# Fixed places for the experts' matmul groups beside the scans, and slots of their own for each kind of chunk

## The chip, the core and the metric

The kernel runs on one core of a Trainium2 chip. The metric is device time in microseconds (us) of one execution. A core has five engines with a queue each: TensorE (PE, matmuls), VectorE (DVE), ScalarE (ACT), GpSimd (POOL) and SyncE (SP, which issues most DMAs). Each takes its queue in order; a waiting instruction holds up all behind it.

## The reference: what is computed

The input is 2 batches x 256 channels x 4096 positions, float32. Layer 0 is a group norm and a Mamba block with 256 inner channels. Layer 1 is a layer norm and two Mamba blocks with 512 inner channels each, one over reversed time, and after them a mixture of 8 experts with softmax weights. The parts that matter, cut:

```python
# Mamba block: projections, causal conv of 4 taps, then a scan over time for 16 states per channel
xs, z = split(x @ W_in);  xs = silu(conv(xs))
dt = softplus(dbc[..., :16] @ W_dt + b_dt);  B, C = dbc[..., 16:32], dbc[..., 32:]   # dbc = xs @ W_x
h[t] = h[t-1] * exp(dt[t] * A) + dt[t] * xs[t] * B[t]
y = sum_s(h * C) + xs * D;  out = (y * silu(z)) @ W_out
# experts, each for every position, weighed by a softmax over mean features
h = relu(bn(x @ W1[e]));  h = relu(bn(h @ W2[e]));  y = sum_e w[e] * (h @ Wo[e] + bo[e])
```

## The kernel before

**Chunks, quads and slots.** Time is cut into 8 chunks of 512 positions. The six Mamba jobs run one after another: batch 0 layer 0 ("narrow"), batch 0 forward, batch 0 backward, then the same three of batch 1. A narrow chunk has 2 blocks of 128 channels, a forward or backward ("wide") chunk 4. The scans of a block are done in 4 quads of 2 scans each, and one scan is one **slot**: 16 slots in a narrow chunk, 32 in a wide one, 1280 in all. A place in a chunk is called p0 to p15 or p0 to p31 here; `n` is the quad modulo 8 and `h` the half, so p = 2n + h in a narrow chunk.

**What a slot holds.** In each slot ACT makes the decays of the next slot (`emit_decay`, line 752, two ACTIVATEs into PSUM, after a small join, line 763), DVE scans (`emit_scan`, line 778) and, unless `on_pool`, multiplies the states by C (line 787). POOL makes the scans' input (`emit_b`, line 742, 128x2048) and for some quads multiplies by C (line 803). PE sums the states into `y` (`emit_sum`, line 811) in the slots that `SUMS` names; `emit_skip` (818) opens a `y`, `emit_gate` (824) closes it.

**What lies beside the scans.** The next chunks are prepared in the same slots, by a table of slots relative to a chunk's start, `SLOTS`: the `xs` products (458) and their ACT copies (515), the convolution `conv` (531, tanh 540, DVE 544), `dbc` (559), `dt` (582, three ACTIVATEs 589 to 591, DVE 594, POOL 598, two stores), the gate's product `z` (458, tanh 621, DVE 624), and the out products of the chunk just scanned, `out` (841, 843, ACT copy 858, store 859). `preload_act_table_set` (660) switches ACT's table between the logarithm's and the tanh's set. `norm` does layer 1's layer norm for the forward jobs, `features` the one ahead of the experts, once a backward chunk is out. Batch 1's narrow chunks are prepared during batch 0's forward chunks and kept in DRAM (`AHEAD_SLOTS`). All these products use a pool of three PSUM banks (`psp`); a product whose bank is not yet read waits for the bank's reader.

**The experts' items.** When a chunk's features are there, its 8 experts can run. One item is (batch, chunk, expert): three layers (line 992) of two groups, a group being two matmuls that run as four passes, with an ACT step each (1005, 1001). `experts` is a planner: it walks over all slots, keeps estimates of PE's and ACT's arrears (`behind`, `act_behind`, against `PE_ROOM`, `PE_BEHIND`, `ACT_ROOM`, `ACT_BEHIND`), and puts up to five groups in a slot if the arrears, the layers' order (`follows`) and the three banks (`fits`) allow it. Groups are emitted in the queue `pe2`, behind the slot's sums. What is left when the scans end is computed in a second stage, the **tail** (`layer`, 1326, and `last_layer`, 1350), where DVE also weighs and adds the items that were computed early (1275, 1276).

**Order.** `Slots` keeps a list of functions for each slot and queue; the main loop runs, slot by slot, `sp`, then `pe`, the sums, `pe2`, the carry and decays, `act`, `dve0`, the scan, `dve`, and `pool`. `in_order` fixes this order on every engine. Weights of a layer of an item are asked for on SP 3 slots after the last use of their buffer by the item before.

Of the kernel before, what the change touches and what calls it, by code (L numbers as in the profile page):

```python
# [64 lines left out]
SUMS = {(0, 0): (-1,), (2, 0): (0, 1), (4, 0): (2, 3), (6, 0): (4,), (7, 0): (5, 6)}  # L65
# [7 lines left out]
    2: dict(xs=(-23, -22), conv=(-20,), dbc=-16, dt=(-14, -13), z=(-10, -9), out=(7, 8)),  # L73
    4: dict(
        xs=(-31, -30, -24, -23), conv=(-26, -21), dbc=-17, dt=(-15, -13, -11, -9), z=(-6, -5, -3, -2),
        out=(16, 18),
    ),
}
AHEAD = 3
AHEAD_SLOTS = dict(x=-7, scale=-5, xs=(-1, 0), conv=(2,), dbc=10, dt=(14, 22), z=(-4, 12))  # L80
# [5 lines left out]
PE_ROOM, PE_BEHIND = 3.8, 2.5  # L86
ACT_ROOM, ACT_BEHIND = 2.6, 1.2
# [5 lines left out]
class Scan:  # L93


    def __init__(self, params, din, batch, layer, flip):
        self.params, self.din, self.nj = params, din, din // P
        self.batch, self.layer, self.flip = batch, layer, flip

# [6 lines left out]
class Slots:  # L106


    QUEUES = ("sp", "pe", "act", "dve0", "dve", "pool", "pe2")

    def __init__(self):
        self.at = {}

        self.products, self.acts, self.banks = {}, {}, []

    def count(self, slot, products=0, acts=0, banks=()):
        self.products[slot] = self.products.get(slot, 0) + products
        self.acts[slot + 1] = self.acts.get(slot + 1, 0) + acts
        self.banks.extend((slot, slot + n, 1) for n in banks)
# [17 lines left out]
def hybrid_kernel(ctx: ExitStack, tc: tile.TileContext, a: dict, out: bass.AP):  # L137
# [56 lines left out]
    with ExitStack() as st:  # L194
# [159 lines left out]

        def norm(i):
# [83 lines left out]
            late = 1 if NCH < i < 2 * NCH else 0  # L439
            for d, queue, fn in (  # L440
                (-48, "sp", load_x), (-44, "pe", mean), (-43, "dve", centre), (-42, "act", square),
                (late - 41, "pe", variance), (late - 40, "act", roots), (late - 39, "dve", divide), (late - 39, "pool", add),
                (-35 if c else -38, "act", affine), (-34, "sp", store),
            ):

                sl.put(s0 + d + (6 if c == 0 else 0), queue, fn)
            s0 += 6 if c == 0 else 0
            sl.count(s0 - 44, 2, 0, (1,))
            sl.count(s0 - 43, 0, 1)
            sl.count(s0 - 41, 2, 4, (2,))  # L450
            sl.count(s0 - 40, 0, 0, (1,))
            sl.count(s0 - (36 if c else 39), 0, 2.3)
# [11 lines left out]
        def prepare(i):  # L464

            (job, c), ck, tag, s0 = steps[i], cks[i], tags[i], starts[i]
            nj, at = job.nj, SLOTS[job.nj]
            if NCH < i <= 2 * NCH + 1:
                at = dict(at, xs=(-31, -29, -24, -23), log=-18)
            ahead = job is jobs[AHEAD]  # L470
            at_rows = slice(XC, 2 * XC) if ahead else slice(0, XC)
# [49 lines left out]
            def conv(jp):  # L521
                v, th = {}, {}

                def pe():
                    for r in range(2):
                        v[r] = psp.tile([P, T], F32, tag="ps", name=f"conv_{tag}_{jp}{r}")

                    for k in range(5):
                        for r, col, j in TILES:
                            rows = slice(64 * r, 64 * r + 64)  # L530
                            nc.tensor.matmul(  # L531
                                v[r][64 * col : 64 * col + 64, :], job.matrices["conv"][rows, 2 * jp + j, k, :],
                                ck["xs", jp][rows, j, k : k + T] if k < 4 else one_col[rows, :].to_broadcast([P // 2, T]),
                                start=(k == 0), stop=(k == 4),
                            )

                def act(r):
                    j = 2 * jp + r
                    th[r] = wk.tile([P, T], F32, tag="th", name=f"thx_{tag}_{j}", bufs=3)
                    nc.scalar.activation(th[r], v[r], AF.Tanh)  # L540

                def dve(r):
                    j = 2 * jp + r
                    nc.vector.scalar_tensor_tensor(
                        of_chunk("xc", j, 6, "eh1"), th[r], 1.0, v[r], ALU.add, ALU.mult
                    )

                return (
                    (0, "pe", pe), (1, "act", lambda: act(0)), (2, "act", lambda: act(1)),
                    (2, "dve0", lambda: dve(0)), (3, "dve0", lambda: dve(1)),  # L550
                )
# [25 lines left out]
            def softplus(j):  # L577
# [22 lines left out]
                def store(key):  # L600
# [7 lines left out]
                    (0, "pe", pe), (1, "act", act), (2, "dve", dve), (2, "pool", pool),  # L608
# [3 lines left out]
            def gate(j):  # L612

                v = {}

                def pe():
                    v["ps"] = in_proj(job, ck, 1, j, f"z_{tag}_{j}")

                def act():
                    v["th"] = wk.tile([P, T], F32, tag="th", name=f"thz_{tag}_{j}", bufs=3)  # L620
                    nc.scalar.activation(v["th"], v["ps"], AF.Tanh, scale=0.5)

                def dve():
                    nc.vector.scalar_tensor_tensor(  # L624
                        of_chunk("sz", j, 8, "eu"), v["th"], 1.0, v["ps"], ALU.add, ALU.mult
                    )

                return (0, "pe", pe), (1, "act", act), (2, "dve", dve)
# [5 lines left out]
            if c == 0:  # L634
                load_weights(job, tag, s0)
                sl.put(s0 + SLOTS[nj]["xs"][0], "act", lambda: start_job(job, tag))
# [10 lines left out]
            for j in range(nj):  # L647
                put(at["xs"][j], xs(j))
                sl.count(s0 + at["xs"][j], 2, 1, (1,))
                put(at["dt"][j], softplus(j))  # L650
                sl.count(s0 + at["dt"][j], 1, 3, (2,))
                sl.count(s0 + at["z"][j], 2, 1, (2,))
            for jp in range(nj // 2):
                put(at["conv"][jp], conv(jp))
                sl.count(s0 + at["conv"][jp], 5, 1, (1, 2))
                sl.count(s0 + at["conv"][jp] + 1, 0, 1)
            put(at["dbc"], x_proj())
            sl.count(s0 + at["dbc"], nj, 1, (1,))
            for slot, table in () if ahead else ((at.get("log", at["dt"][0]), "natural_log_exp_and_others"), (at["z"][0], "exp_and_others")):
# [166 lines left out]
        def finish(i):  # L826
# [25 lines left out]

            slots = SLOTS[2 if i == AHEAD * NCH - 1 else job.nj]["out"] if i + 1 < len(steps) else (3, 4)
            for slot in slots:
                sl.count(s0 + slot, 1 + job.nj, 1, (1,))
            for m, slot in enumerate(slots):
                sl.put(s0 + slot, "pe", lambda m=m: project(m))
# [5 lines left out]
        def features(b, c, v, s0):  # L863
# [29 lines left out]
            for d, queue, fn in (  # L893
                (0, "pe", mean), (1, "dve", centre), (2, "act", square), (4, "pe", variance),
                (5, "act", lambda: rsqrt(v["var"], v["var"], eps5)), (6, "dve", divide),
                (7, "sp", lambda: nc.sync.dma_start(nf_dram[b][:, c, :, :], v["cen"])),
            ):
                sl.put(s0 + d, queue, fn)
            sl.count(s0, 2, 0, (1,))
            sl.count(s0 + 1, 0, 2)  # L900
            sl.count(s0 + 4, 2, 2, (2,))
            ready.append((s0 + 9, b, c))
# [24 lines left out]
        def experts():  # L927

            last = 2 * nq + 15
# [11 lines left out]
            def sums_in(slot):  # L941
                n, h = divmod(slot % 16, 2)
                return 1.25 * len(SUMS.get((n, h), ())) + (1 if (n, h) in ((2, 0), (6, 0)) else 0)

            todo = [(at, b, c, e) for at, b, c in sorted(ready) for e in range(E)]
            behind = act_behind = 0.0
            times = [[], [], []]

            def follows(l):
# [4 lines left out]
                waits = [(l - 1, k * KC + 1, 2)] if l else []  # L954
# [11 lines left out]
            for slot in range(last):  # L966
                behind = max(0.0, behind) + sl.products.get(slot, 0) + sums_in(slot) - PE_ROOM
                act_behind = max(0.0, act_behind) + sl.acts.get(slot + 1, 0) - ACT_ROOM
                for l in (2, 1, 1, 0, 0):
                    at = follows(l)  # L970
                    if at is None or slot < at:
                        continue
                    if behind + 2 > PE_BEHIND or act_behind + 1.3 > ACT_BEHIND or not fits(slot):
                        break
                    banks.insert(sum(b[0] <= slot for b in banks), (slot, slot + 1, 0))
                    times[l].append(slot)
                    behind += 2
                    act_behind += 1 if l == 2 else 1.3
# [4 lines left out]
            emit_experts(put)  # L983

        def emit_experts(put):
# [40 lines left out]
            for b, c, e, times in put:  # L1026
# [5 lines left out]
                sl.put(times[0], "pe2", lambda b=b, c=c, key=key: key.update(n=n[b, c]))  # L1032
                for l, (x, dst) in enumerate((("n", "h1"), ("h1", "h2"), ("h2", "u"))):
                    at = before.get(l, times[0] - 6) + 3
                    sl.put(at, "sp", lambda l=l, e=e, key=key: load_w(l, e, key["tag"]))
                    for m in range(KC):
                        slot = before[l] = times[l * KC + m]
                        pe, act = layer(x, dst, l, m, e, key)
                        sl.put(slot, "pe2", pe)
# [49 lines left out]
        at_first = SLOTS[2]["xs"][0] - 3  # L1089
# [15 lines left out]
        for g in range(nq):  # L1105
            i, jp, n = quads[g]
            for h in range(2):
# [3 lines left out]

                if (n, h) in ((2, 0), (6, 0)):
# [17 lines left out]
                if (n, h) in ((1, 0), (5, 0)) and done:  # L1130
                    emit_gate(*done.pop(0))
# [450 lines left out]
```

## Time and profile before

| what | us |
|---|---|
| median of 3 runs (lowest, highest) | 4978.65 (4976.32, 4984.62) |
| the profiled execution's own time | 4972.65 |
| its span, first to last instruction | 4970.9 |
| first scan starts, last scan ends | 58.1, 4439.8 |
| starts of batch 0 forward, backward | 525.8, 1418.9 |
| starts of batch 1 narrow, forward, backward | 2280.1, 2710.6, 3580.5 |

The page gives busy time by engine, the span in 40 slices, the chain that ended last and the costliest groups of instructions. The stages' borders are the starts of their first scans, counted off in the timeline of DVE (the scans are line 778). A view by windows gives each engine's busy time between two moments, the number of its instructions, and the share of TensorE's clock that was granted; a window's length less an engine's busy time is its idle time.

### The profile page before, as it was taken

How to read it: one execution, taken by the hardware profiler on the slowest of the kernel's cores; microseconds unless marked ns; L12 is line 12 of the kernel's file. 1: busy time of each engine (PE TensorE's matmuls, PEld its weight loads, DVE VectorE, ACT ScalarE, POOL GpSimd, SP SyncE). 2: the span in 40 equal slices, each digit the busy share in tenths (PEclk: the TensorE clock that was granted, in tenths of full speed). 3: DMA queues.
4: the chain of work that ended last, by engine and by line, in shares of the span. 5: the costliest groups of instructions: out<-in, count | busy, mean ns of one | idle time of the engine just before them, and what ended most of it. 6: DMA issues, size and time to landing. Idle time of an engine off the chain costs nothing. (4 is left out here: it accounts for less than half of the span.)

```text
span 4970.9 us, 47346 instructions
## 1 busy us (share of the span) xinstructions
PE 4225.8 (85%) x14912; PEld 1476.1 (30%) x14912; DVE 4567.6 (92%) x3097; ACT 3613.1 (73%) x7304; POOL 4340.4 (87%) x1424
## 2 busy tenths in 40 slices
PE   5777777788776899989999899889868989999999
PEld 1222222222222233333333333333222333334444
DVE  6998999999999999999999999999999999975565
ACT  5777777777777788878788788888767888862232
POOL 6998999999999999999999999999999999960000
PEclk8778899989988999999999999999989999999999
DMA  5455454444444455446676555555534455536653
GB/s 193 158 184 171 154 171 158 158 145 155 164 157 148 173 183 177 165 174 237 241 246 222 170 173 170 189 169 190 175 121 153 165 187 176 186 131 233 226 168 127
DMA packets 335407, 875.26 MB, mean 176 GB/s; under 512 B 36314, under 2 KB 111860, under 8 KB 293172
## 3 DMA queue, kind: packets, MB, share of 16 engines
q1 hardware_dynamic: 326164, 835.39, 48.7%
q0 software_dynamic: 8992, 36.85, 2.9%
q8 instruction: 118, 1.93, 0.2%
q14 instruction: 133, 1.09, 0.1%
HBM read 673.27 MB, written 198.84 MB: 175 GB/s over the span
## 5 line engine op out<-in xcount | busy, mean ns | idle before, releaser
L742 POOL TENSOR_TENSOR bq<-rxdt,bc 128x2048 f32<-128x2048 f32 x640 | 2893.8, 4544 | 15.2 <-DMA rxdt<-xdtd 7.3
L752 ACT ACTIVATE da<-rdt,w_a 128x512 f32<-128x512 f32 x2560 | 1756.9, 686 | 70.0 <-DVE bq L778 23.6
L778 DVE TENSOR_TENSOR_SCAN da<-da,h_state,bq 128x1024 f32<-128x1024 f32 x664 | 1557.9, 2346 | 50.3 <-ACT da L752 34.7
L803 POOL TENSOR_TENSOR bq<-bq,bc 128x2048 f32<-128x2048 f32 (+1 forms) x280 | 1180.1, 4215 | 22.6
L778 DVE TENSOR_TENSOR_SCAN bq<-da,h_state,bq 128x1024 f32<-128x1024 f32 x456 | 1059.0, 2338 | 8.1 <-ACT da L752 7.9
L811 PE MATMUL y<-bq,stack 128*32 128x512 f32 x5120 | 742.2, 665 | 276.5 <-POOL bq L803 251.2
L787 DVE TENSOR_TENSOR bq<-da,bc 128x1024 f32<-128x1024 f32 x760 | 926.2, 1219 | 15.7
L992 PE MATMUL e<-eh,ew 128*128 128x512 f32 x1376 | 659.5, 613 | 43.3 <-DVE sp L594 14.4
L797 ACT COPY h_state<-da 128x2 f32<-128x2 f32 x759 | 119.0, 157 | 618.8 <-DVE bq L787 615.4
L763 ACT ACTIVATE bq<-h_state,bq,a 128x1 f32<-128x1 f32 x1120 | 430.0, 384 | 4.7 <-POOL bq L742 4.1
L811 PEld LDWEIGHTS y<-bq,stack 128*32 128x32 f32 x5120 | 140.6, 116 | 823.7 <-POOL bq L803 373.6
L458 PE MATMUL z<-nx,w_in 128*128 128x512 f32 x640 | 332.6, 650 | 59.3 <-DVE q L423 21.0
L992 PEld LDWEIGHTS e<-eh,ew 128*128 128x128 f32 x1376 | 247.7, 191 | 450.4 <-issue 240.5
L531 PE MATMUL conv<-xs,w_conv 64*64 64x512 f32 x2560 | 334.6, 603 | 22.7 <-ACT xs L515 20.4
L992 PE MATMUL e<-en,ew 128*128 128x512 f32 x688 | 324.8, 605 | 26.5 <-DVE xr L891 17.6
L458 PE MATMUL xs<-nx,w_in 128*128 128x512 f32 x640 | 318.9, 626 | 31.2 <-DVE sz L624 18.4
L1330 ACT ACTIVATE h<-hp,of,sc 128x512 f32<-128x512 f32 x168 | 130.6, 777 | 275.2 <-PE hp L1326 273.7
L843 PE MATMUL o<-sz,w_out 128*128 128x512 f32 x640 | 295.8, 601 | 0.0
L1005 ACT ACTIVATE eh<-e,of,sc 128x512 f32<-128x512 f32 x344 | 260.1, 768 | 47.3 <-PE e L992 46.9
L598 POOL TENSOR_TENSOR xdt<-sp,xc 128x512 f32<-128x512 f32 x160 | 203.2, 1274 | 43.6 <-DVE sp L594 43.6
L778 DVE TENSOR_TENSOR_SCAN da<-da,bq 128x1024 f32<-128x1024 f32 x96 | 219.4, 2285 | 2.6 <-issue 1.5
L458 PEld LDWEIGHTS z<-nx,w_in 128*128 128x128 f32 x640 | 125.1, 205 | 262.1 <-issue 147.8
(145 smaller groups left out, 4753.5 us busy)
## 6 DMA issues: line engine op xcount, KB each, us to landing
rxdt<-xdtd SPq DMA_DIRECT2D x160, 1024.0 KB, 6.0
rdt<-dtd SPq DMA_DIRECT2D x160, 1024.0 KB, 6.8
bc<-bcd SPq DMA_DIRECT2D x384, 256.0 KB, 3.2
ew<-in_W SPq DMA_DIRECT2D x172, 256.0 KB, 4.9
u<-u SPq DMA_DIRECT2D x86, 512.0 KB, 5.7
u<-eu SPq DMA_DIRECT2D x82, 512.0 KB, 4.4
dtd<-sp SPq DMA_DIRECT2D x160, 256.0 KB, 3.3
xdtd<-xdt SPq DMA_DIRECT2D x160, 256.0 KB, 3.4
```

The source lines that it names most:

```text
L458: nc.tensor.matmul(ps, job.matrices["in", half][:, k, j * P : (j + 1) * P], rhs, start=(k == 0), stop=(k == KC - 1),)
L531: nc.tensor.matmul(v[r][64 * col : 64 * col + 64, :], job.matrices["conv"][rows, 2 * jp + j, k, :], ck["xs", jp][rows, j, k : k + T] if k ...
L742: nc.gpsimd.tensor_tensor(bq[g], ck["rxdt", j], over_groups(ck["bc", 0, sg]), ALU.mult)
L752: nc.scalar.activation(da[g, h][:, k, :], cks[i]["rdt", j][:, q, :], AF.Exp, scale=steps[i][0].w["a"][:, j, q * SG + sg : q * SG + sg + 1],)
L763: nc.scalar.activation(bq[g][:, q, 0:1], job.h[:, j, sg, q : q + 1], AF.Identity, scale=cks[i]["a0", j][:, h, sg : sg + 1], bias=bq[g][:, ...
L778: nc.vector.tensor_tensor_scan(b if on_pool(g, h) else d, d, b, job.h[:, j, sg, 2 * h : 2 * h + 1] if c else 0.0, ALU.mult, ALU.add,)
L787: nc.vector.tensor_tensor(bq[g][:, two, :], d, cks[i]["bc", 1, sg].rearrange("p (o t) -> p o t", o=1).to_broadcast([P, 2, T]), ALU.mult,)
L803: nc.gpsimd.tensor_tensor(b, b, cks[i]["bc", 1, sg].rearrange("p (o t) -> p o t", o=1).to_broadcast([P, groups, T]), ALU.mult,)
L811: nc.tensor.matmul(y[i, j][q * CG : (q + 1) * CG, :], stack, bq[g][:, q, :], start=False, stop=(sg == SG - 1),)
L843: nc.tensor.matmul(v[m], job.w["out"][:, j, m * P : (m + 1) * P], ck["sz", j], start=False, stop=(j == job.nj - 1),)
L992: nc.tensor.matmul(ps, ew[l][:, k, m * P : (m + 1) * P], key[x][:, k, :], start=(k == 0), stop=(k == KC - 1),)
L1005: nc.scalar.activation(key[dst][:, m, :], key["ps", l, m], AF.Relu, bias=of[:, l, e, m : m + 1], scale=sc[:, l, e, m : m + 1],)
```

## The change

Fixed tables take the planner's place, and each kind of chunk has tables of its own.

- `PLACES` says for each kind of chunk how many groups a slot may hold, and by its sign where: negative in a new queue `pe1` ahead of the slot's sums and other products, positive in `pe2` behind them. The order of layers and the three banks still decide, too. The estimates of arrears and their `count`s are gone; `hold` keeps the banks' part.
- `SLOTS` is now by kind. Narrow: `xs` a slot earlier (-24, -23), `conv` a slot earlier, the second `dt` a slot later, `z` at (-8, -9) in place of (-10, -9), `out` at (6, 9) in place of (7, 8). Forward: `z` in the order (-6, -3, -5, -2), `out` two slots later. Backward: the last `z` four slots later, at +2. The switch to tanh's table has a slot of its own, `tanh`. Batch 0's forward chunks 1 to 7 and backward chunks 0 and 1 keep the old slots (`UNDER_AHEAD`).
- `norm` of batch 1's forward chunks 1 to 7 is one to two slots earlier (`NORM`); `features` has its square one slot later and its store two.
- `WHEN`, `GATES` and `APART` name values that stay as they were.

```diff
 SLOTS = {
-    2: dict(xs=(-23, -22), conv=(-20,), dbc=-16, dt=(-14, -13), z=(-10, -9), out=(7, 8)),
-    4: dict(
-        xs=(-31, -30, -24, -23), conv=(-26, -21), dbc=-17, dt=(-15, -13, -11, -9), z=(-6, -5, -3, -2),
-        out=(16, 18),
-    ),
+    "l0": dict(xs=(-24, -23), conv=(-21,), dbc=-16, dt=(-14, -12), z=(-8, -9), tanh=-6, out=(6, 9)),
+    "fwd": dict(xs=(-31, -30, -24, -23), conv=(-26, -21), dbc=-17, dt=(-15, -13, -11, -9), z=(-6, -3, -5, -2), tanh=-3, out=(18, 20)),
+    "bwd": dict(xs=(-31, -30, -24, -23), conv=(-26, -21), dbc=-17, dt=(-15, -13, -11, -9), z=(-6, -5, -3, 2), tanh=-4, out=(16, 18)),
 }
+UNDER_AHEAD = dict(xs=(-31, -29, -24, -23), conv=(-26, -21), dbc=-17, log=-18, dt=(-15, -13, -11, -9), z=(-6, -5, -3, -2), tanh=-6, out=(16, 18))
+NORM = (-50, -45, -44, -43, -42, -41, -40, -34, -32)
+NORM_0 = (-48, -44, -43, -42, -40, -39, -38, -35, -34)
+FIRST_NORM = (-43, -38, -37, -36, -35, -34, -33, -32, -29)
+FEATURES = (0, 1, 3, 4, 5, 6, 9)
+PLACES = {
+    "l0": (1, 1, 0, -2, 1, -2, -1, -2, 0, 0, 2, 1, 0, 1, 2, 0),
+    "fwd": (1, 1, 1, 1, 1, 0, 2, -2, 1, 0, 1, 1, -1, 2, 1, 1, -1, -2, 2, -1, 2, 0, -1, 1, 1, 1, 1, 1, 1, 1, 1, 1),
+    "bwd": (1, 1, 1, 1, 1, 0, 1, 1, -1, 1, 1, 0, 1, 1, 0, 1, 1, -1, 1, 1, 2, -1, 2, -1, -1, -1, 1, 0, 1, -2, 1, -1),
+}
...
-            for slot, table in () if ahead else ((at.get("log", at["dt"][0]), "natural_log_exp_and_others"), (at["z"][0], "exp_and_others")):
+            for slot, table in () if ahead else ((at.get("log", at["dt"][0]), "natural_log_exp_and_others"), (at["tanh"], "exp_and_others")):
...
-            for slot in range(last):
-                behind = max(0.0, behind) + sl.products.get(slot, 0) + sums_in(slot) - PE_ROOM
-                act_behind = max(0.0, act_behind) + sl.acts.get(slot + 1, 0) - ACT_ROOM
-                for l in (2, 1, 1, 0, 0):
-                    at = follows(l)
-                    if at is None or slot < at:
-                        continue
-                    if behind + 2 > PE_BEHIND or act_behind + 1.3 > ACT_BEHIND or not fits(slot):
-                        break
...
+            for i, (job, _) in enumerate(steps):
+                for p in range(8 * job.nj if i + 1 < len(steps) else 8 * job.nj + 15):
+                    slot = starts[i] + p
+                    free = abs(PLACES[job.kind][p]) if p < 8 * job.nj else 1
+                    for l in (2, 1, 1, 0, 0):
+                        at = follows(l)
+                        if at is None or slot < at:
+                            continue
+                        if not free or not fits(slot):
+                            break
+                        banks.insert(sum(b[0] <= slot for b in banks), (slot, slot + 1, 0))
+                        times[l].append(slot)
+                        front[slot] = p < 8 * job.nj and PLACES[job.kind][p] < 0
+                        free -= 1
...
-                        sl.put(slot, "pe2", pe)
+                        sl.put(slot, "pe1" if front[slot] else "pe2", pe)
...
                 sl.run(slot, "sp")
                 flush(slot)
 
+                sl.run(slot, "pe1")
                 if (n, h) in ((2, 0), (6, 0)):
                     emit_skip(i, 2 * jp + n // SG)
                 sl.run(slot, "pe")
```

## The prediction, as it was put on record

> **What bounds it now.** I read the page first, then idle time by stage, then who ended the waits in the two narrow stages, then one narrow chunk in order of time, and last the chain that ended last.
>
> ```profile
> span 4970.9 us, 47346 instructions
> PE 4225.8 (85%) x14912; PEld 1476.1 (30%) x14912; DVE 4567.6 (92%) x3097; ACT 3613.1 (73%) x7304; POOL 4340.4 (87%) x1424
> ```
>
> The table by windows (columns: window, its length, then busy time with number of instructions of PE, weight loads, DVE, ACT, POOL, then granted clock, DMA share, GB/s) has the six jobs and the tail:
>
> ```profile
> 58.10:525.80 467.70, 327.89 (x1168) 101.77 (x1168) 443.79 (x305) 342.86 (x704) 441.92 (x143) 0.81 0.52 177
> 525.80:1418.90 893.10, 696.10 (x2766) 216.32 (x2767) 877.49 (x600) 686.27 (x1435) 879.91 (x292) 0.90 0.48 159
> 1418.90:2280.10 861.20, 743.82 (x2743) 255.16 (x2742) 846.60 (x546) 677.38 (x1388) 855.55 (x271) 0.94 0.48 169
> 2280.10:2710.60 430.50, 397.02 (x1285) 145.83 (x1284) 407.08 (x241) 349.03 (x705) 417.68 (x127) 0.96 0.70 241
> 2710.60:3580.50 869.90, 782.63 (x2870) 268.39 (x2868) 855.36 (x557) 712.28 (x1453) 861.55 (x278) 0.96 0.54 176
> 3580.50:4439.80 859.30, 736.37 (x2704) 253.84 (x2700) 842.85 (x540) 669.57 (x1369) 846.07 (x269) 0.94 0.46 161
> 4439.80:4970.90 531.10, 510.81 (x1266) 222.56 (x1264) 276.23 (x274) 150.19 (x201) 28.78 (x41) 0.99 0.55 186
> ```
>
> Length less busy gives POOL's idle time: 25.8, 13.2, 5.7, 12.8, 8.4 and 13.2 us in the six jobs (7.9 of the last at its very end), DVE's: 23.9, 15.6, 14.6, 23.4, 14.5, 16.5. Both engines are full at once, and the change takes none of their instructions away in the scans. So a better order can win only idle time. A steady backward chunk (window 4120.0 to 4227.8) has 0.6 idle on POOL and 1.2 on DVE, and 9.8 on PE: nothing to win there. The tail is PE's: 510.81 of 531.10.
>
> **The tail: +10.6.** Laid side by side, the two programs' orders of instructions hold 86 and 85 early items (516 and 510 groups). One more is left to the tail. Its price is a round of the chain that ended last:
>
> ```profile
> 4562.49 4.29 PE hp L1326 x10
> ...
> 4569.63 3.43 PE y L1350 x8
> 4573.07 4.29 PE hp L1326 x10
> ```
>
> 4573.07 - 4562.49 = 10.58 us for one item's 24 passes. DVE loses 2 x 1.2 us of adding an early item and gains one weighing; it is idle for half of the tail, so neither counts. Behind the last scan come 10 groups in place of 9. A group is 4 passes of 0.43, 1.7 us, but PE waits 2.2 us for the tail's first weights there; I take 0 (to +1.7).
>
> **Batch 0's narrow chunks: +6.** No experts run here; only the slots move. In the chunk at 286.4, in order of time:
>
> ```profile
> 312.96 0.58 ACT L858 COPY xr<-o 128x512 f32<-128x512 f32 x1
> 313.38 0.67 DVE L624 SCALAR_TENSOR_TENSOR sz<-thz,z 128x512 f32<-128x512 f32 x1
> 314.11 2.07 PE L841 MATMUL o<-xr,ident 128*128 128x512 f32 x2 [7.44 <-DVE sz L624]
> 318.62 0.59 ACT L858 COPY xr<-o 128x512 f32<-128x512 f32 x1 [1.66 <-PE o L843]
> 320.37 3.70 PE L458 MATMUL xs<-nx,w_in 128*128 128x512 f32 x8
> 322.39 0.59 ACT L515 COPY xs<-xs 128x512 f32<-128x512 f32 x1 [1.33 <-PE xs L458]
> 324.66 2.36 DVE L778 TENSOR_TENSOR_SCAN da<-da,h_state,bq 128x1024 f32<-128x1024 f32 x1 [0.40 <-issue]
> ```
>
> The second out product stands 7.44 us until DVE has read a z bank; it ends at 318.51; ACT, in order, waits for it and for the xs product, so the decay of p12 is late and the scan waits 0.40 (1.17 in the chunk before). After the change the z readers are on p9 and p10. Without a reader on p8, scan 9 starts at 314.5 and its reader ends at 314.5 + 2.26 + 0.67 = 317.4. The out product then takes 4.4 as here (314.11 to 318.51) or 2.6 as its sister did without a pause before it (302.21 to 304.79), and ends at 321.9 or 320.0. On p10 ACT has its copy (0.59), the table load, now on p10 (1.28), and the one xs copy that is left (0.59 + 0.20 for the edges; its product ends 1.85 after the out product), then join and decays (1.6): 326.2 or 324.4. The scan of p12 is due at 324.2 (scans 9, 10 and 11 with their followers: 3.98 + 3.46 + 2.26). It is 2.0 or 0.2 late, against 0.4 to 1.2 now. The convolution, a slot earlier, only follows. The difference lies between -1.0 and +1.6 a chunk; PE still pauses before that product and the granted clock of this chunk is 0.78, so I go toward the slow row: +1.0 in 6 chunks, +6 (-6 to +10).
>
> [...]
>
> **Batch 1's narrow chunks: -5.** The first six hold 15 to 19 groups each today, 12 after; the last two 11 and 7, then 11 and 3. PE goes from 397 of 430.5 busy to about 397 - 35 x 1.7 = 337. DVE's waits in this stage are for decays that ACT makes late behind PE:
>
> ```profile
> DVE da L778 <- ACT da L752: 13.9, 15, 4.9
> ```
>
> The longest, 4.9, comes from a group that waits 4.8 for its last layer's weights; such loads are asked for 3 slots after the buffer's last use, and reuse after only 4 slots occurs 60 times today, 22 times after. But POOL idles only 12.8 here, 8.0 of it in the last two chunks, which hardly change. The most is 12.8 less 8 half-steady chunks at 0.3 = 10.4. I take 5 (from -10 to +3, if late groups now meet the same spots).
>
> **Wide chunks: -1.** Steady chunks hold 18 groups before and after; only places move, with PE idle 9.8 a chunk, so 0. Batch 1's first two backward chunks go from 1 and 0 groups to 19 and 16; PE idles 33 and 32 us in them, the 34 groups cost 58, and the like chunks of batch 0 (108.0 with 18 groups) are not longer than these (104.9 and 110.9): 0 (-1 to +4). The last chunk of both backward jobs goes from 33 groups to 26: -1 (-4 to 0). Batch 1's forward norm spreads the four root steps away from a softplus on the same slot: 0 (-3 to +5).
>
> **Queues.** ACT gets 31 more table loads, 111 for 80, for tanh now comes before its switch and the switch then loads the same set again: 31 x 1.283 = 39.8 us of ACT time. In the backward chunk the second load meets a wait of 1.31 us for DVE before a carry (at 1947.66) and the first is the old one moved, so I take 0; the narrow one is counted above; with the cover gone it is 40. [...]
> On SP, `out` moves the store of the residual into the slot where the next one is loaded into the same buffer (p11 narrow, p22 forward). SP then stands until the store has landed, 3.1 us in 24 chunks, with softplus stores and `bc`, `rxdt`, `rdt` loads behind it. These are asked for 9 to 12 slots (30 us and more) ahead and land in 3 to 7: 0; uncovered, 74. The norm's load and the features' store only move along empty slots.
>
> **Sum.** 10.6 + 6 - 5 - 1 = +10.6. On the profiled execution: 4972.65 + 10.6 = 4983.3. That execution is 6.0 under the median of the runs, so I put it on the median: 4978.65 + 10.6 = 4989.3.
>
> **Rivals.** Measurement can tell about 0.2%, 10 us.
> A, the sum above, chance 0.40; own range +4 to +20, about a third of it under +10.
> B, faster: the waits in both narrow stages and at the borders of jobs go. The idle time over the steady level is 23 (batch 0 narrow), 10 (batch 1 narrow) and some 4 elsewhere; two thirds of it, 25, less 10.6: -14, 4964. For it: those waits are ACT behind PE, and the change takes groups out of there. Against: batch 0's narrow chunks have none. It decides if the narrow stages shorten by over 20. Chance 0.28.
> C, slower by more: the same SP and ACT additions come through. All narrow chunks at their slow end (+10), a third of the table loads (13), -3 elsewhere and the tail: +31, 5010. It decides if DVE idles over 1.6 in a steady wide chunk. Chance 0.13.
> D, no difference: the tables name places, but layer order, buffers and banks decide as before, and what the tail costs the narrow chunks of batch 1 give back: 0, 4979. Chance 0.19.
>
> Faster 0.28 (B); same 0.19 + 0.14 of A = 0.33; slower 0.26 + 0.13 = 0.39. The range leaves out B's far third (0.09) and most of C (0.1): 4960 to 5003.
>
> **What would show it.** The last scan's end: A has it at about 4439.8 + 0, B before 4420, C after 4455. The tail from there: 531 to 542. Narrow stages: 467.7 becomes 474, 430.5 becomes 425; B has 450 and 420. DVE's idle in steady wide chunks stays at 1 to 2. The out product's wait for `sz` in a narrow chunk shrinks from 7.4 to about 2. I am wrong if the tail grows by less than 8, or if a stage of wide chunks moves by over 5.

## The result, and the profile after

The changed kernel takes 4986.76 us (median of 20 runs, 4981.08 to 4997.69) against 4978.61 (20 runs) for the kernel before on the same chip: ratio 1.0017, 95% interval 1.0010 to 1.0024. That is 8 us slower, and just under the 0.2% named as the bound. The profiled execution's span is 4979.3 us, 8.4 more than before.

The page's first lines: PE, DVE and POOL are as busy as before. ACT has 37 us more: its table loads are 130 for 99, of 1.283 us each.

```profile
span 4979.3 us, 47353 instructions
...
PE 4229.9 (85%) x14912; PEld 1462.2 (29%) x14912; DVE 4564.4 (92%) x3096; ACT 3650.0 (73%) x7333; POOL 4340.2 (87%) x1424
```

The table by windows, same columns as before, cut at the changed kernel's own borders:

```profile
58.40:517.10 458.70, 327.86 (x1168) 95.41 (x1168) 444.02 (x305) 353.82 (x712) 440.19 (x143) 0.84 0.53 181
517.10:1414.20 897.10, 703.41 (x2767) 216.68 (x2768) 877.97 (x601) 686.53 (x1435) 880.25 (x292) 0.89 0.47 159
1414.20:2278.50 864.30, 738.21 (x2723) 247.94 (x2721) 846.28 (x546) 680.44 (x1388) 857.68 (x271) 0.94 0.48 166
2278.50:2698.90 420.40, 346.85 (x1144) 120.62 (x1144) 405.97 (x241) 328.79 (x672) 413.20 (x127) 0.94 0.66 225
2698.90:3565.60 866.70, 780.32 (x2886) 272.77 (x2887) 854.36 (x556) 725.05 (x1465) 862.18 (x278) 0.97 0.54 180
3565.60:4431.60 866.00, 775.12 (x2820) 267.37 (x2818) 842.53 (x540) 695.10 (x1406) 847.40 (x269) 0.97 0.49 168
4431.60:4979.30 547.70, 526.32 (x1288) 229.05 (x1288) 275.29 (x273) 153.41 (x205) 28.88 (x41) 0.98 0.52 179
```

Both narrow stages are shorter (467.7 to 458.7, 430.5 to 420.4), both backward stages longer (861.2 to 864.3, 859.3 to 866.0), the tail longer by 16.6. One profile each can mislead, so here is every stage over all profiles that share it, the experiments' too. Terms of the change are differences of these means:

| stage | before, 2 profiles | changed, mean (profiles; lowest, highest) | difference | predicted |
|---|---|---|---|---|
| batch 0 narrow | 467.7, 467.2 | 459.3 (9; 458.6, 461.3) | -8.1 | +6 |
| batch 0 forward | 893.1, 897.7 | 898.1 (12; 895.6, 900.5) | +2.7 | |
| batch 0 backward | 861.2, 860.0 | 865.7 (8; 864.1, 868.3) | +5.1 | wide in all: -1 |
| batch 1 narrow | 430.5, 433.9 | 420.8 (9; 419.3, 422.6) | -11.4 | -5 |
| batch 1 forward | 869.9, 870.0 | 868.1 (9; 866.7, 869.6) | -1.8 | |
| batch 1 backward | 859.3, 859.1 | 867.4 (6; 862.2, 871.5) | +8.2 | |
| tail | 531.1, 535.1 | 545.3 (7; 541.5, 547.7) | +12.2 | +10.6 |

The sum is some +6.8. The difference of batch 0's forward stage is within what two profiles of the same kernel differ by.

How the out product's wait in batch 0's narrow stage went is seen in the chunk at 282.6, in order of time:

```profile
312.55 0.58 ACT L633 ACTIVATE thz<-z 128x512 f32<-128x512 f32 x1
312.94 0.67 DVE L636 SCALAR_TENSOR_TENSOR sz<-thz,z 128x512 f32<-128x512 f32 x1
...
313.66 1.13 PE L852 MATMUL o<-xr,ident 128*128 128x512 f32 x2 [1.41 <-DVE sz L636]
314.63 1.88 PE L854 MATMUL o<-sz,w_out 128*128 128x512 f32 x4
...
316.34 1.88 PE L471 MATMUL xs<-nx,w_in 128*128 128x512 f32 x4
...
317.15 1.28 ACT L671 ACT_TABLE_LOAD   x1
...
320.93 2.36 DVE L789 TENSOR_TENSOR_SCAN da<-da,h_state,bq 128x1024 f32<-128x1024 f32 x1 [0.50 <-issue]
```

The second out product waits 1.41 us for `sz`, not 7.44. After so short a pause it takes 2.85 us (313.66 to 316.51, granted clock 1.00) in place of 4.40 (0.62); xs follows at once. This chunk still comes out even, 54.7 us for 54.6: its scan of p12 is 0.50 late, for 0.40 before. Counted by chunk over the nine profiles, the -8.1 is -2.1, -0.5, +0.1, -1.2, +0.4, -2.9, -2.0 and 0.0. In chunks 0, 1 and 3 the scan of p12 had been 1.2 to 1.3 late. In chunk 5 the shorter wait counts most. There the product `mean` of `norm` stands in PE's queue behind the out and the xs products, and DVE waited for it, first before, then after:

```profile
368.67 2.08 PE L841 MATMUL o<-xr,ident 128*128 128x512 f32 x2 [7.43 <-DVE sz L624]
...
378.50 1.88 PE L399 MATMUL mean<-nx,columns 128*128 128x512 f32 x4
...
380.41 1.22 DVE L404 TENSOR_TENSOR nx<-nx,mean 128x1024 f32<-128x1024 f32 x1 [2.34 <-PE mean L399]
...
371.62 1.98 PE L416 MATMUL mean<-nx,columns 128*128 128x512 f32 x4
...
373.75 1.19 DVE L421 TENSOR_TENSOR nx<-nx,mean 128x1024 f32<-128x1024 f32 x1
```

In chunk 6 DVE's wait for the convolution's tanh falls from 3.5 to 2.1.

The chain that ended last still goes round in the tail in 10.58 us an item (4613.00 - 4602.42):

```profile
4602.42 4.29 PE hp L1332 x10
...
4609.57 3.43 PE y L1356 x8
4613.00 4.29 PE hp L1332 x10
```

### The profile page after: what moved, and what is told of

The parts are those of the page before. It is cut to its first block, busy times and chain, and to the rows that moved or that the text cites. A ratio compares the mean times of both kernels' runs of the same rounds, so it can differ in the third digit from the quotient of the medians.

```text
span 4979.3 us, 47353 instructions
## 1 busy us (share of the span) xinstructions
PE 4229.9 (85%) x14912; PEld 1462.2 (29%) x14912; DVE 4564.4 (92%) x3096; ACT 3650.0 (73%) x7333; POOL 4340.2 (87%) x1424
## 5 line engine op out<-in xcount | busy, mean ns | idle before, releaser
L997 PE MATMUL e<-eh,ew 128*128 128x512 f32 x1360 | 674.2, 625 | 54.4 <-DVE xc L556 18.9
L997 PE MATMUL e<-en,ew 128*128 128x512 f32 x680 | 336.0, 619 | 48.6 <-DVE xr L901 21.7
L829 PE MATMUL y<-xc,w_d 128*128 128x512 f32 x320 | 182.3, 653 | 29.5 <-DVE sz L835 29.5
```

The source lines that it names most:

```text
L997: nc.tensor.matmul(ps, ew[l][:, k, m * P : (m + 1) * P], key[x][:, k, :], start=(k == 0), stop=(k == KC - 1),)
```

## The experiments

Ratios are to the kernel before, run on the same chip. Stage times are from one profile each.

**The kernel before, again.** No edit.

> The kernel before once more, for a second profile: how far do its stages scatter? Four kernels with the changed kernel's tail (two items more or none apart) had tails of 541.5, 543.0, 546.2 and 547.7 us. Theory A: the kernel before scatters in the same way, so its tail is anywhere from 530 to 537 and the change's own step in the tail is the one item, 10.6 (536.6 by the mean of the other four less 544.6). Theory B: the tail of before is steady at 531 (530 to 532) and the change costs some 13 to 14 there, more than the item. For batch 0's forward stage (893.1 here, 896.6 to 900.4 in five profiles of kernels with the changed order, though its slots are the same): within 1 us of 893 if the change did something there, 896 or more if it is scatter.

Tail 535.1, batch 0 forward 897.7. Theory A: both scatter by 4 us in one and the same kernel. Seven tails of 85 items have a mean of 545.3, so the change costs 12.2 there.

**Old slots for batch 0's narrow chunks.**

```diff
+L0_0 = dict(xs=(-23, -22), conv=(-20,), dbc=-16, dt=(-14, -13), z=(-10, -9), tanh=-10, out=(7, 8))
...
         def kind_of(i):
+            if i < NCH:
+                return L0_0
```

> The changed kernel with batch 0's narrow chunks alone given back their old slots (all of them: xs, conv, dt, z, out, and the table switch on the slot of the first z); the experts' places and all other jobs stay as changed. Theory: the 9.0 us that batch 0's narrow stage lost (467.7 to 458.7) come from the new slots of z and out, which let the second out product run soon after a busy stretch; then this stage goes back to 467 (465 to 470), all other stages stay within 3 us, and the whole is about 9 us over the changed kernel (4988 of profiled span). Rival 1: the 9 us are scatter between two executions, since the stage holds no experts; then it stays at 459 (457 to 461). Rival 2: it is the earlier xs and conv that did it; this run does not tell it from the theory, a further one would.

The stage is back, to a tenth. By windows, this kernel:

```profile
59.10:526.60 467.50, 327.27 (x1168) 102.17 (x1168) 443.66 (x305) 343.87 (x705) 441.17 (x143) 0.81 0.52 176
```

The granted clock falls from 0.84 to 0.81 with it, but e5_one_load has 0.81 too and keeps 458.6, so the mean clock of the stage doesn't tell where the time goes. Rival 1 is out. The whole came to 1.0022 (1.0014 to 1.0031), 2.5 us over the changed kernel's ratio and not 9; the two intervals leave room up to 8. The stage is settled by this, the whole is not: this profile's batch 1 backward stage (862.2) and tail (541.5) are the lowest of their kind, and I can't say whether by chance.

**Only z, switch and out old there.**

```diff
+L0_0 = dict(xs=(-24, -23), conv=(-21,), dbc=-16, dt=(-14, -12), z=(-10, -9), tanh=-10, out=(7, 8))
```

> The changed kernel with only z, the table switch and out of batch 0's narrow chunks at their old slots; xs, conv and dt stay a slot earlier or later, as changed. Theory: these alone made the 9 us, so the stage is back at 466 to 468 (e1_old_narrow_b0, with all slots old: 467.5). Rival: xs and conv, a slot earlier, made part of it; then it lies between 460 and 465.

477.0, outside both: with the new xs and conv the old z and out cost 18 us, more than the old set as a whole. The waits of that stage in this kernel (engine, line, waited for: us in total, times, longest):

```profile
DVE sz L838 <- PE y L825: 11.4, 5, 3.3
DVE da L792 <- POOL h_state L816: 6.0, 5, 1.4
...
PE o L855 <- DVE sz L639: 25.7, 5, 5.5
```

The out product waits 25.7 us in all for `sz` (42.5 in the kernel before, 6.3 in the changed one), and DVE's gate now waits 11.4 us for the sums of `y` (2.6 before). I take it that the conv, a slot earlier, stands with the out product ahead of these sums. So the gains of single edits don't add: the new xs, conv and dt alone cost 9.5 us (467.5 to 477.0), the new z, switch and out on top of them win 18. The new z and out with the old xs and conv were not run, so how the 8.1 are shared isn't shown.

**One table switch.** Two kernels: `tanh` on the slot of the first z product, a slot ahead of the first tanh; and on the slot of the first tanh itself.

```diff
-    "l0": dict(xs=(-24, -23), conv=(-21,), dbc=-16, dt=(-14, -12), z=(-8, -9), tanh=-6, out=(6, 9)),
+    "l0": dict(xs=(-24, -23), conv=(-21,), dbc=-16, dt=(-14, -12), z=(-8, -9), tanh=-9, out=(6, 9)),
...
```

The first has `tanh` at -9, -6 and -6 in narrow, forward and backward chunks, the second at -8, -5 and -5.

> The changed kernel with the switch to tanh's table put on the slot of the first tanh again in all three kinds of chunk, so that 31 table loads fall away (80 in place of 111, 39.8 us of ACT time); nothing else moves. Theory, as predicted: they are hidden beside waits of ACT; every stage stays within 2 us and the whole within 3 us of the changed kernel. Rival: ACT is short in the backward stages, and the 6.6 us that batch 1's backward stage gained are these loads; then both backward stages fall by 3 to 7 us, the forward one of batch 1 by 0 to 3, and the whole is 6 to 15 us under the changed kernel.

> The changed kernel with the switch to tanh's table on the slot of the first tanh and just ahead of it: the order of all engines is that of the changed kernel, and only table loads fall away (net 30 of 130 on the page's count of all loads, 30 x 1.283 = 38.5 us of ACT time). In e2_one_switch the switch stood a slot earlier still, so that run mixed two things. Theory, as predicted: the loads are hidden, and the whole is within 3 us of the changed kernel; batch 0's narrow stage stays at 458 to 460, so that the 5.3 us of e2_one_switch there came from the earlier slot of the switch. Rival: ACT is short where the second load stands; then batch 0's narrow stage and the backward stages fall by 2 to 5 us each.

1.0019 (1.0009 to 1.0029) and 1.0019 (1.0010 to 1.0028): as the changed kernel. In the second, where nothing else moves, batch 0's narrow stage stays at 458.6, and no stage is shorter than in the other profiles of the table (900.5 and 871.5 are the longest of theirs): 38.5 us of loads were hidden, as predicted. In the first, batch 0's narrow stage is 464.0: a switch one slot too early costs 5 (in three chunks the scan interval at p8 goes from 2.26 to 3.36), a load too many nothing.

**All groups behind.**

```diff
-                        front[slot] = p < 8 * job.nj and PLACES[job.kind][p] < 0
+                        front[slot] = False
```

> The changed kernel with every place of an experts' group behind the slot's sums and products; none stands ahead of them. Number, slots and items stay as they are. Theory: the side counts little, since TensorE idles in every stage; each stage stays within 3 us of the changed kernel, and the whole within 5. Rival: a group behind a product that waits for a PSUM bank waits with it, and ACT's step for it comes too late for the next decays; then batch 1's narrow stage rises from 420.5 to 425 or more, and the two wide stages of batch 1 by 5 us each: 10 to 25 us over the changed kernel.

1.0024 (1.0015 to 1.0034); 421.1, 866.9 and 870.5 in batch 1's stages: the theory. The sign in the table is worth nothing measurable; the slots stayed as they were.

**Old wide slots, new places.**

```diff
-    "fwd": dict(xs=(-31, -30, -24, -23), conv=(-26, -21), dbc=-17, dt=(-15, -13, -11, -9), z=(-6, -3, -5, -2), tanh=-3, out=(18, 20)),
-    "bwd": dict(xs=(-31, -30, -24, -23), conv=(-26, -21), dbc=-17, dt=(-15, -13, -11, -9), z=(-6, -5, -3, 2), tanh=-4, out=(16, 18)),
+    "fwd": dict(xs=(-31, -30, -24, -23), conv=(-26, -21), dbc=-17, dt=(-15, -13, -11, -9), z=(-6, -5, -3, -2), tanh=-6, out=(16, 18)),
+    "bwd": dict(xs=(-31, -30, -24, -23), conv=(-26, -21), dbc=-17, dt=(-15, -13, -11, -9), z=(-6, -5, -3, -2), tanh=-6, out=(16, 18)),
```

> The changed kernel with the old slots of z, out and the table switch in batch 1's forward chunks and in the backward chunks; places, norm and features stay as changed. The items come out at 84 in place of 85, with 8 groups after the last scan in place of 10. Theory: the new wide slots are worth little, about -1 to +1 us in batch 1's forward stage and 0 in the backward ones; the tail grows by 10.6 for the item and loses some 3 for two groups: the whole is 5 to 10 us over the changed kernel. Rival: the backward z at +2 is what makes the backward stages longer (batch 1's from 859.3 to 862 to 869 in five profiles); then both backward stages fall by 3 to 6 and the whole comes out even with the changed kernel.

1.0098 (1.0085 to 1.0112). Both were wrong. The backward stages stay long (866.5, 866.0), so their slots are not the cause. Batch 1's forward stage grows by 25.7; in its chunks 1 to 6 DVE waits for

```profile
DVE sz L835 <- PE y L822: 12.3, 6, 2.1
DVE da L789 <- ACT da L763: 10.7, 13, 1.4
```

once 2 us a chunk for the last sum of a `y`, and then for decays; it is p18 that grows, from 3.99 to 7.67. The new places put groups on p15 and p16, and the old out products stand on p16 and p18. So the new places go with the new slots. Which of z, switch and out it is, this run doesn't tell, for it moved them together. The tail with 84 items is 556.9.

**Crowded narrow chunks.**

```diff
-    "l0": (1, 1, 0, -2, 1, -2, -1, -2, 0, 0, 2, 1, 0, 1, 2, 0),
+    "l0": (1, 1, 1, -2, 1, -2, -1, -2, 1, 1, 2, 1, 1, 1, 2, 1),
```

> The changed kernel with a place in every slot of the narrow chunks (the five zeros of the table become ones): batch 1's first six narrow chunks hold 16 to 20 groups in place of 12, and what they take is missing in batch 1's first two backward chunks (0 in place of 19 and 16). Early items stay 85, so the tail stays. Theory: the 10.1 us that batch 1's narrow stage lost come from fewer groups there; then it goes from 420.5 back to 429 or more, and batch 1's first two backward chunks lose the 4.7 us that they gained; the whole is 4 to 8 us over the changed kernel. Rival: the places (none beside the out products, none beside the carries) count and not the number; then the narrow stage comes out at 421 to 424, and the whole falls by 2 to 5 us.

1.0083 (1.0071 to 1.0095): the stage takes 455.6, 35 more. The direction is the theory's, the size is four times what I expected. Waits in this stage:

```profile
DVE da L789 <- ACT da L763: 20.2, 13, 8.3
DVE bq L789 <- ACT da L763: 16.9, 10, 4.0
...
PE e L997 <- DMA ew<-in_Wo: 18.8, 9, 7.8
PE e L997 <- DMA ew<-in_W: 14.6, 2, 9.0
```

PE waits 33 us for the experts' weights, ACT in order behind it, and DVE 37 us for ACT. The changed kernel has 7.5 and 6.6 of these. Batch 1's first backward chunk, which has no groups here, takes 103.5 us; with its 19 or 20 groups it takes 107.9 to 110.0.

**Two weight buffers, crowded.** On the two edits of the crowded and the dense kernel:

```diff
...
-                    sl.put(at, "sp", lambda l=l, e=e, key=key: load_w(l, e, key["tag"]))
+                    turn = len(used.setdefault(l, [])) % 2 if l != 1 else 0
+                    if l != 1 and len(used[l]) > 1:
+                        at = used[l][-2] + 3
+                    sl.put(at, "sp", lambda l=l, e=e, key=key, turn=turn: load_w(l, e, key, turn))
...
```

> The crowded narrow places of e4_crowded_narrow_b1 and the dense last chunk of e3_dense_last, with a second buffer for the weights of the experts' first and third layers, so that these are asked for an item earlier. Batch 1's narrow stage: 455.6 in e4_crowded_narrow_b1, 420.8 by the changed table, 430.6 and 433.9 in two profiles of the kernel before. TensorE waits there 33.4 us for the experts' weights in the crowded kernel, 7.5 in the changed one, 7.3 in the kernel before, and VectorE 37.1, 6.6 and 16.4 for decays that come late behind them. Theory: crowding costs by weights that come late, not by the groups themselves; with the second buffers the waits for the weights of these two layers go (below 8 us in all), and the stage falls to 420 to 432. The whole is then 0.996 to 0.998 of the kernel before. Rival: the groups themselves make ScalarE late, wherever their weights are; then the stage stays above 440 with the waits for weights gone.

437.2: between the two. Half of the 35 us went with the waits for weights:

```profile
DVE da L789 <- ACT da L763: 9.9, 11, 3.8
DVE bq L789 <- ACT da L763: 6.7, 3, 4.8
...
PE e L997 <- DMA ew<-in_W: 4.1, 1, 4.1
```

The other 16 us stay, and DVE still waits 16.6 for ACT with nearly all weights there. So late weights are about half of what crowding costs; what the other half is, this run doesn't show. The whole is 1.0015 (1.0006 to 1.0024), not under 1 as expected.

**A dense last chunk.**

```diff
-                    free = abs(PLACES[job.kind][p]) if p < 8 * job.nj else 1
+                    free = (2 if i + 1 == len(steps) else abs(PLACES[job.kind][p])) if p < 8 * job.nj else 1
```

> The changed kernel with two places in every slot of the very last chunk (batch 1 backward, chunk 7) in place of its table: 38 groups there in place of 26, 87 early items in place of 85. Theory: the tail is one chain of TensorE, two items fewer are worth 2 x 10.6 = 21 us, and somewhat more if pauses go with them: the tail falls from 547.7 to 524 to 527. The last chunk gains 0 to 5 us, since TensorE idles about 10 us in a steady one but 12 groups take 20; the whole is 16 to 21 us under the changed kernel, and so under the kernel before as well. Rival: TensorE is full in that chunk, so 12 more groups lengthen it by 12 to 20 us, and the whole moves by less than 6.

0.9977 (0.9967 to 0.9988): faster than both kernels. The tail and the last chunk of this kernel:

```profile
4440.40:4966.40 526.00, 507.80 (x1250) 220.97 (x1248) 277.16 (x276) 148.63 (x199) 28.95 (x41) 0.98 0.55 189
4332.80:4440.40 107.60, 99.00 (x315) 37.80 (x312) 100.02 (x58) 84.47 (x167) 92.58 (x29) 1.00 0.44 148
```

Twelve more groups lengthen the last chunk by some 2.5 us (108.2 on the mean of three kernels with them, 105.7 without), and three tails with 87 items (526.0, 523.2, 523.2) lie 21.1 under the seven with 85: 10.6 an item, the row's price. No chunk is prepared there any more, and PE and ACT had room: with the twelve groups they are busy for 99.0 and 84.5 of 107.6 us, in the changed kernel for 91.4 and 78.3 of 105.5.

**Weights asked for a slot earlier**, with the dense last chunk.

```diff
-                    at = before.get(l, times[0] - 6) + 3
+                    at = before.get(l, times[0] - 6) + 2
```

> The changed kernel with the dense last chunk of e3_dense_last, and the weights of a layer asked for 2 slots after the last use of their buffer in place of 3. Places, slots and orders of all other engines stay. In seven profiles with the changed places, batch 0's backward stage takes 864 to 868 us and batch 1's 862 to 872, against 860 and 859 in two of the kernel before; steady chunks differ by two events: up to 4.5 us more in the first two slots, where a group of layer 0 waits for weights whose buffer was last used 4 slots earlier, and 1.6 us more at p11 and p12 in about every third chunk. Theory: the first event is the late load; asked a slot earlier it goes (the first two scans take 4.5 us in every steady chunk), the second stays; each backward stage falls by 1 to 4 us, and the whole comes to 0.996 to 0.9975 of the kernel before (e3_dense_last had 0.9977). Rival: SP, in order, now stands until the buffer is free and holds what is behind it (bc, rdt, rxdt), so stages get longer by 2 us or more, or the event stays.

0.9977 (0.9968 to 0.9986), the same as without. The theory's event is real: in the profile of e5_one_load it looks like this, in order of time (the scan is that of the second slot):

```profile
4007.53 3.40 PE L997 MATMUL e<-en,ew 128*128 128x512 f32 x4 [4.11 <-DMA ew<-in_W]
...
4010.97 0.78 ACT L1010 ACTIVATE eh<-e,of,sc 128x512 f32<-128x512 f32 x1 [6.37 <-PE e L997]
...
4011.98 1.41 ACT L763 ACTIVATE da<-rdt,w_a 128x512 f32<-128x512 f32 x2
...
4013.42 2.35 DVE L789 TENSOR_TENSOR_SCAN bq<-da,h_state,bq 128x1024 f32<-128x1024 f32 x1 [4.38 <-ACT da L763]
```

It occurs in 24 of 72 steady backward chunks of eight profiles (batch 0's chunks 3 to 6, batch 1's 2 to 6), and in none of the 18 of the two kernels that ask earlier. Yet the load was not asked for late. SP issued it 12 us before PE had it:

```profile
3994.08 0.51 SPq L701 DMA_DIRECT2D rxdt<-xdtd  x1
3994.69 0.54 SPq L907 DMA_DIRECT2D nf_dram<-xr  x1
3995.33 0.40 SPq L1019 DMA_DIRECT2D ew<-in_W  x1
```

The change moved the store of `features` (`nf_dram<-xr`) by two slots. It now follows the 1 MB load of `rxdt`, which came behind it before, and the experts' weights follow the store. Size and median time from issue to landing, before and after:

```profile
nf_dram<-xr SPq DMA_DIRECT2D x15, 512.0 KB, 4.0
nf_dram<-xr SPq DMA_DIRECT2D x15, 512.0 KB, 8.7
```

The weights right behind the store land in 6.7 to 10.1 us in the changed kernel's steady chunks, in 12.1 in the chunk above. Asked for a slot earlier, they go ahead of the load of `rxdt` and the store. No run moved the store alone.

Over the 72 chunks the event is worth 0.4 us each. That is less than the changed kernel wins at the same place: its first two scans take 4.5 us where no load is late, in the kernel before 5.1 in every steady chunk. And asking earlier may cost something itself: batch 0's chunk 2 takes 112.7 us in both kernels that do it, 108.5 to 111.1 in the other eight.

**The backward jobs as before**, with the dense last chunk.

```diff
-FEATURES = (0, 1, 3, 4, 5, 6, 9)
+FEATURES = (0, 1, 2, 4, 5, 6, 7)
...
+    "steady": (1, 1, 0, 2, 0, 1, 0, 1, 0, 1, 1, 0, 1, 1, 1, 1, 0, 0, 0, 0, 0, 0, 1, 0, 0, 1, 1, 0, 1, 1, 0, 2),
```

The backward line of `SLOTS` is the old one, as in the edit above, and "steady" holds for backward chunks 0 to 6.

> The changed kernel with the dense last chunk, and the backward jobs put back: old slots of z and of the table switch, old features, and a table of places that gives batch 0's backward chunks the groups where the kernel before has them (but for one, at p15 in place of p26); 86 early items. Theory: the 5 to 8 us that each backward stage took longer come from its places, above all the group at p8 that waits for a PSUM bank beside xs, and the one at p30 whose weights come late; so batch 0's backward stage is back at 860 to 862 and no steady chunk shows the two events. Batch 1's first two backward chunks still cost some 3 us more than in the kernel before, for their groups. The tail is one item longer than that of e3_dense_last, 536. The whole is 0.997 to 0.998 of the kernel before. Rival: it is the sheer groups in batch 1 and scatter in batch 0; then batch 0's backward stage stays at 864 to 868.

1.0001 (0.9992 to 1.0010). Both events (the late load, and one at p11 and p12 that is shown below) are gone, in every steady chunk, as the theory had it; with the old `FEATURES` the store lands in 4.1 us again. Yet batch 0's stage stays at 867.2: in six of nine steady chunks p17 to p19 now take 12.1 us or more in place of 10.5, two slots behind the one group that had to go on p15. That loss is this run's own, so it doesn't tell by itself whether the two events were all that was lost.

## Why the prediction was right, and where it was not

The forecast, +10.6 and 4989.3, is 2.5 us from the measured 4986.76, and case A came. It was right by cancellation: of its four terms one was right, one had the wrong size, and two the wrong sign. By its own tests ("I am wrong if ... a stage of wide chunks moves by over 5") the reasoning had failed where the sum had not.

**The tail, +10.6:** right. With 84, 85, 86 and 87 items the changed places give tails of 556.9, 545.3, 531.2 (e9_old_backward) and 524.1: 10.9 an item on the mean. With the kernel before's 86 items the tail is as long as its own (531.1, 535.1), so the item is what was lost. The rest of the 12.2 is within the scatter; the tenth group behind the last scan makes the tail's first product start 0.5 us later (29.4 for 28.9 us after that scan). 16.6 in the profile was scatter.

**Batch 0's narrow chunks, +6:** wrong in sign, -8.1. The step that failed: "PE still pauses before that product and the granted clock of this chunk is 0.78, so I go toward the slow row". The 0.78 is the mean over the whole chunk in the kernel before. The pause right before the product fell from 7.44 us to 1.41, and behind it the product took 2.85 us at a granted clock of 1.00, near the fast row's 2.6 and not the slow row's 4.4 (granted clock 0.62). With the fast row my own range had -1.0 a chunk, -6 in six. That this also comes near the size is luck: chunks 0 to 4, the kind that I had worked out, make 3.2 of the 8.1, and chunks 5 and 6 make 4.9 by waits of DVE (for `mean` and for a tanh) that I had not looked at.

**Batch 1's narrow chunks, -5:** right in sign, -11.4 in size. I took half of 10.4, the idle time of POOL over a steady level. DVE's waits for ACT's decays fell from 16.4 (13.9 and 2.5) to 6.6 by themselves:

```profile
DVE da L789 <- ACT da L763: 5.4, 9, 3.4
DVE bq L789 <- ACT da L763: 1.2, 2, 0.9
```

The crowded kernel shows that groups in this stage cost far more than idle time tells: a late weight stops PE, then ACT, then DVE (33 us of waits for weights on PE, 37 us for decays on DVE, 35 us of the stage). By chunk, 6.3 of the 11.4 came in the one that had held 20 groups, 2.3 in the first, and 3.8 in the last two, of which I had said that they "hardly change"; why these two won, no run shows.

**Wide chunks, -1:** failed, +11.5 (+5.1, -1.8 and +8.2; batch 0's forward stage left out as scatter). The step: "only places move, with PE idle 9.8 a chunk, so 0". PE's idle time was no room where a group's place made ACT late: at 4010.97 above ACT stood 6.37 us for PE, and DVE's next scan 4.38 for ACT. Of the 8.2 in batch 1, 3.8 are its first backward chunk (19 groups where 1 was; in my range), 3.7 its five steady chunks, 1.8 its last, which has fewer groups than before, and the second wins 1.0. Of batch 0's 5.1, four steady chunks have 2.5, chunk 2 has 1.6 and the last 1.4. The steady chunks have two events that the kernel before never shows. One is the late load above. The other, in two chunks of e3_dense_last, first without and then with it:

```profile
4139.70 1.98 PE L997 MATMUL e<-eh,ew 128*128 128x512 f32 x4 [1.38 <-DVE xc L556]
...
4152.31 2.33 DVE L789 TENSOR_TENSOR_SCAN da<-da,h_state,bq 128x1024 f32<-128x1024 f32 x1
...
4248.16 3.27 PE L997 MATMUL e<-eh,ew 128*128 128x512 f32 x4 [1.92 <-DVE xc L556]
...
4261.44 2.36 DVE L789 TENSOR_TENSOR_SCAN da<-da,h_state,bq 128x1024 f32<-128x1024 f32 x1 [0.59 <-issue]
```

The group at p8 waits for a PSUM bank that DVE reads. After the longer pause its four passes run slowly (granted clock 0.58, in the other chunk 1.00), and p11 and p12 take 8.0 us in place of 6.4. In 90 steady chunks of ten profiles with these places this happened 24 times. Each time, and only then, the first product behind the pause took over 2.4 us for 1.98: 20 times the group, and 4 times, in e6_all_behind, the xs product that goes ahead of it there.

In batch 1's five steady chunks the late loads make 2.4 of the 3.7 and the slow passes 1.3. The first of the five loses another 1.2 at p18, in every profile, and the rest of the new order wins 0.3 a chunk.

**Queues, 0:** right for the table loads, which are hidden (e5_one_load). SP's stands for the residual's store came about as priced, 67 us in 23 waits (74 foreseen); no stage shows that they cost anything, but no run took them away. The step that failed is the last: "The norm's load and the features' store only move along empty slots". The store lands in 8.7 us for 4.0, SP stands 107 us for it (3 before), and the weights behind it are the late load.

**B** had both narrow stages shorter (19.5 us, near its 20), and the backward stages and the tail took that back. **C** didn't come: the table loads cost nothing, the narrow stages went the other way; of SP's stands only the features' store shows a cost.

Open: what the backward chunks lose at p18 and in the last chunk, what the 16 us of crowding without late weights are, and why batch 0's chunk 2 is 4 us longer where weights are asked for earlier.

## What to carry over

Price a moved piece of work by what waits in order behind it, not by the idle time of its own engine: here a group of 1.7 us, on the wrong slot, cost 1.6 us of scan time in one chunk and nothing in the next. Ask of a moved transfer what it now stands behind, and what stands behind it: a store two slots later took 8.7 us for 4.0, and the weights with it. Fixed places and the slots of the other work are one design, and undoing half of it (477.0, 893.8) is worse than either whole. Work that a tail would do at its full price of 10.6 us an item goes first where nothing is being prepared: the last chunk took twelve more groups for 2.5 us.

## What the hardware showed

TensorE's clock after short pauses: at p8 of the 90 steady backward chunks of these ten profiles, 32 pauses of 1.02 to 1.84 us were all followed by four passes in 1.98 us (in the changed kernel, after 1.60 us, at a granted clock of 1.00). Of 58 pauses of 1.91 to 2.62 us, 24 were followed by slow ones (2.41 to 3.68); over the slow four shown above the granted clock is 0.58. The length of such a pause alone did not tell which: in two chunks of the changed kernel, one after the other, 2.61 us (to 1980.90) was followed by 1.98 at 1.00, and 2.33 us (to 2088.56) by 2.89 at 0.66. What else decides it, no run here shows.

PE's queue in its order: while the out product stood 7.44 us in the kernel before (306.67 to 314.11), PE ran nothing, and the products behind it started at 315.98, 318.51 and 320.37.

ACT's table loads take 1.283 us each, all 130 in the changed kernel. They begin 0.017 to 0.019 us after the end of the instruction before them, and 101 of them are followed after 0.011 to 0.013. In e5_one_load 30 of them fewer left the time unchanged (1.0019 of the kernel before, for the changed kernel's 1.0017).

Transfers on SP's queue: 512 KB stored ahead of a 1 MB load landed in 4.0 us in the kernel before (median of 15), right behind it in 8.7 in the changed one.
